# Query-by-query layout of the transposed tiles in a pre-norm retention and FP4-FFN layer

## The chip, the cores and the metric

The kernel runs on one core of one Trainium2 chip. The metric is the device time of one launch in microseconds. The core has five engines that run side by side and wait for each other through semaphores: TensorE (PE in the profile; its weight loads are the rows PEld), VectorE (DVE), ScalarE (ACT), GpSimd (POOL) and SyncE (SP), which here only issues DMAs.

## What is computed

The reference takes X of 8 sequences with 2048 rows of 256 values, all float32, and computes one layer:

```python
x = x + attn(layernorm(x), W_Q, W_K, W_V)
x = x + ffn(layernorm(x), w_gate, w_up, w_down)
# attn: Q = xpos(X @ W_Q); K = xpos(X @ W_K, downscale); V = X @ W_V
#       (softmax(Q K^T) * 0.9**|n-m|) @ V, softmax over all 2048 keys
# ffn:  down(silu(gate(x)) * up(x)); 704 hidden values; input and weights of each
#       linear are first rounded to FP4 (E2M1) values in blocks of 16
```

The decay 0.9**|n-m| is so small far from the diagonal that the kernel multiplies probabilities with V only in the key blocks at most 7 blocks of 128 away from the query block. The softmax's maximum and sum go over all keys.

## The kernel before

Work is done in blocks of 128 query rows (P = 128); there are 8 x 16 = 128 of them, and one call of `step(n)` for each. Groups of four blocks (GROUP = 512 rows) are loaded, normalized, transposed and projected ahead of time; keys and values of a whole sequence stay in SBUF. The instruction order of each engine is written out by hand in `step` (the tile framework's scheduling is set to manual), and the framework only adds the semaphores. A step works on several blocks at once, each at another stage. On block n it does the scores (`scores`, L474), the row maximum (`maximum`, L486) and the exponentials (`exponentials`, L507), and it turns the probabilities (`turn_p`). On block n-1 it multiplies the turned probabilities by the decay (`decays`, L547), multiplies them with V (`attend`, L562), adds the residual and normalizes (`add_residual`, `normal_scales`). On block n-2 it rounds the FFN input to FP4 and turns it (`turn_xq`), and runs the gate and up matmuls (`gate_up`, L630). On block n-3 it forms the hidden values, rounds them and turns them (`turn_h`). On block n-4 it runs the down matmuls (`down`, L678) and stores the result. On TensorE a step's order is: scores of n, projections of a later group, down of n-4, attend of n-1, gate and up of n-2. One matmul in float32 shows as two MATMUL and two LDWEIGHTS records in the profile.

TensorE multiplies with the contracted dimension on the partitions, so normalized x, probabilities, the FFN input xq and the hidden values h all have to be transposed. The function `turn` does this without TensorE. DVE's transpose (L238) turns squares of 32 x 32 (SQ = 32, NSQ = 4 squares along each side of a block) within groups of 32 partitions, out of the source into a scratch tile `sq`. ScalarE's queue then issues one DMA of `sq` to a DRAM tile `there` (L244), and SP issues four DMAs back (L247), which move the squares to the partitions where they belong; xq and h come back into the tile they came from. The turned data then lies in the order of the query's group of 32 first, then the block of values, then the query within its group: runs of 32 queries. `in_runs` is the view that names these runs.

Before TensorE uses them, x, xq and h are copied by ScalarE from that order into a tile with each block's 128 queries side by side: `keep_x` (L399, once for a group of four query blocks), `keep_xq` (L616) and `keep_h` (L669). For the probabilities the decay product on DVE (L547) reads the runs and writes the tile `p_t` with the queries side by side. The stationary operand of attend, gate, up and down is a slice of 128 queries of these tiles.

Three of the last blocks have their down matmuls put off to the very end (`deferred`); their turned h is kept in other tiles. The last few blocks are transposed by TensorE into PSUM instead (n of the last two for xq, of the last four for h, the last for the probabilities), and their copies read PSUM. Scores, projections, gate and up share three PSUM buffers (pool ps_s); attend and down share two (ps_m). The tiles h and xq have two buffers each. The changed lines are all in `turn`, the view after it, and the functions that use it.

Of the kernel before, what the change touches and what calls it, by code (L numbers as in the profile page):

```python
# [9 lines left out]
F32 = mybir.dt.float32  # L10
I32 = mybir.dt.int32
AF = mybir.ActivationFunctionType
ALU = mybir.AluOpType
AX = mybir.AxisListType

P = 128
GROUP = 512
BPG = GROUP // P
# [4 lines left out]
SQ = 32  # L23
NSQ = P // SQ
# [10 lines left out]
def preln_xpos_retention_fp4_ffn_kernel(  # L35
# [13 lines left out]
    nc = tc.nc  # L49
    B, L, H = x.shape  # L50
    F = w_gate.shape[0]
    HC = H // P
# [3 lines left out]
    FC = -(-F // P)  # L56
# [4 lines left out]
    ffn_p = ctx.enter_context(tc.tile_pool(name="ffn", bufs=2))  # L61
# [163 lines left out]

    def turn(dst, pieces, name, tag):


        n = sum(src.shape[-1] for src in pieces) // NSQ
        sq = prob_p.tile([P, dst.shape[-1]], F32, tag=tag, bufs=1, name=f"sq_{name}")
        sq = sq[:, : NSQ * n].rearrange("p (c f) -> p c f", c=NSQ)
        at = 0
        for src in pieces:
            w = src.shape[-1] // NSQ
            nc.vector.transpose(  # L238
                sq[:, :, at : at + w].rearrange("p c (k i) -> p k c i", i=SQ),
                src.rearrange("p (k c i) -> p k c i", c=NSQ, i=SQ),  # L240
            )
            at += w
        there = dram.tile([NSQ, SQ, NSQ, n], F32, tag=f"turn_{n}", name=f"there_{name}")
        nc.scalar.dma_start(there.rearrange("a i c f -> (a i) c f"), sq)  # L244
        dst = dst[:, : NSQ * n].rearrange("p (a f) -> p a f", a=NSQ)
        for c in range(NSQ):
            nc.sync.dma_start(dst[ts(c, SQ)], there[:, :, c, :].rearrange("a i f -> i a f"))  # L247

    def in_runs(t):

        return t.rearrange("p (a c i) -> p c a i", a=NSQ, i=SQ)

# [141 lines left out]
    def keep_x(k):  # L396
        xt = groups.pop(k).rearrange("p c d -> p (c d)")
        xn_t = act_p.tile([P, BPG, HC, P], F32, tag="xn_t", bufs=3, name=f"xnt_{k}")
        nc.scalar.copy(  # L399
            xn_t.rearrange("p b h (a i) -> p (b h) a i", a=NSQ), in_runs(xt)  # L400
        )
        normed[k] = xn_t
        load_group(k + 2)

# [117 lines left out]
    def turn_p(n):  # L522
        pieces = exps.pop(n)
        if n == total - 1:
            pt = ps_s.tile([P, HALF, P], F32, tag="s", name=f"pt_p_{n}")
            (pr,) = pieces
            for j in range(pr.shape[-1] // P):
                nc.tensor.transpose(pt[:, j, :], pr[:, ts(j, P)], ident)
            turned[n] = pt.rearrange("p k (a i) -> p k a i", a=NSQ)
        else:  # L530
            runs = prob_p.tile([P, (2 * BAND + 1) * P], F32, tag="runs", bufs=1, name=f"runs_{n}")
            turn(runs, pieces, f"p{n}", "sq")
            turned[n] = in_runs(runs[:, : len(band(n)) * P])


    mid = {}
# [1 line left out]
    def band(n):  # L538
        return [k for half in range(2) for k in keys_of(n, half)]

    def decays(n):
        keys, pt = band(n), turned[n]
        p_t = prob_p.tile([P, 2 * BAND + 1, P], F32, tag="p_t", bufs=1, name=f"p_t_{n}")
        d0 = keys[0] - n % NB + BAND
        for c in range(0, len(keys), BPG):
            to = min(c + BPG, len(keys))
            nc.vector.tensor_tensor(  # L547
                p_t[:, c:to, :].rearrange("p k (a i) -> p k a i", a=NSQ),
                pt[:, c:to],
                decay_sb[:, d0 + c : d0 + to, :].rearrange("p k (a i) -> p k a i", a=NSQ),  # L550
                ALU.mult,
            )
        turned[n] = p_t

# [48 lines left out]
    def turn_xq(n):  # L603
        xq = mid[n][1]
        if n >= total - 2:
            pt = ps_m.tile([P, HC, P], F32, tag="m", name=f"pt_xq_{n}")
            for hc in range(HC):
                nc.tensor.transpose(pt[:, hc, :], xq[:, ts(hc, P)], ident)
            keep_xq(n, pt.rearrange("p c (a i) -> p c a i", a=NSQ))
        else:  # L610
            turn(xq, [xq], f"xq{n}", "sq_x")

    def keep_xq(n, src=None):
        x1, xq, _ = mid[n]
        xq_t = ffn_p.tile([P, HC, P], F32, tag="xq_t", bufs=1, name=f"xq_t_{n}")
        nc.scalar.copy(  # L616
            xq_t.rearrange("p c (a i) -> p c a i", a=NSQ), in_runs(xq) if src is None else src
        )
        mid[n] = (x1, xq_t)

    gated = {}

# [29 lines left out]
    def turn_h(n):  # L652
        h = hid[n][1]
        if n >= total - 4:
            pt = ps_s.tile([P, FC + 2, P], F32, tag="s", name=f"pt_h_{n}")[:, :FC, :]
            for fc in range(FC):
                at = min(fc * P, F - P)
                nc.tensor.transpose(pt[:, fc, :], h[:, at : at + P], ident)
            keep_h(n, pt.rearrange("p c (a i) -> p c a i", a=NSQ))
        else:  # L660
            turn(h, [h[:, : (FC - 1) * P], h[:, F - P : F]], f"h{n}", "sq_h")

    def keep_h(n, src=None):
        x1, h, _ = hid[n]
        if n in deferred:
            h_t = deferred[n][:, : FC * P].rearrange("p (c q) -> p c q", c=FC)
        else:
            h_t = ffn_p.tile([P, FC, P], F32, tag="h_t", bufs=1, name=f"h_t_{n}")
        nc.scalar.copy(  # L669
            h_t.rearrange("p c (a i) -> p c a i", a=NSQ), in_runs(h) if src is None else src  # L670
        )
        hid[n] = (x1, h_t)

    def down(n):
# [67 lines left out]
    def step(n):  # L742
        on = lambda d: 0 <= n - d
        k = NG + n // BPG
        turn_group = (n == 1 or n % BPG == 0 and n > 0) and k < B * NG
        load_residual(n)
        scores(n, 0)
        if on(3):
            hidden(n - 3)
        if on(2):  # L750
            mid[n - 2][2].round()
        if on(3):
            hid[n - 3][2].largest()
        maximum(n, 0)
        weights_in_step(n, "maximum")
        scores(n, 1)
        if decays_first(n):
            decays(n - 1)
        if on(3):
            hid[n - 3][2].normalize()  # L760
        if on(4) and n - 4 < total - 4:
            keep_h(n - 4)
        if on(2):
            turn_xq(n - 2)
        maximum(n, 1)
        exponentials(n)
        if n == 1:
            turn_p(n)
        if on(2) and n - 2 < total - 2:
            keep_xq(n - 2)  # L770
        for g in kept:
            keep_x(g)
        kept.clear()
        weights_in_step(n, "exponentials")
        values = [(g, name) for name, g in parts(n) if name not in ROWS]
        project = lambda: [project_rotated(g, name) for name, g in parts(n) if name in ROWS]
        for g, name in values:
            project_v(g, name)
        if n != 2:
            project()  # L780
        for g, name in values:
            keep_v(g, name)
        if on(1) and not decays_first(n):
            decays(n - 1)
        for name, g in parts(n):
            if n == 1 and name in ROWS:
                rotate(g, name)
        if turn_group:
            if n in (1, BPG):
                statistics(k)  # L790
            normalize_on_scalar(k)
        weights_in_step(n, "decays")
        if on(3):
            hid[n - 3][2].round()
        if on(4) and n - 4 not in deferred:
            down(n - 4)
        if n == 2:
            attend(n - 1)
            project()
        for name, g in parts(n):  # L800
            if n != 1 and name in ROWS:
                rotate(g, name)
        if n > BPG and n % BPG == 1 and k + 1 < B * NG:
            statistics(k + 1)
        if n != 1 and n < total - 1:
            turn_p(n)
        if on(1) and n != 2:
            attend(n - 1)
        weights_in_step(n, "attend")
        for name, g in parts(n):  # L810
            if name in ROWS:
                load_tables()
        if on(4) and n - 4 not in deferred:
            finish(n - 4)
        if on(1):
            inverse_sum(n - 1)
        if n == total - 1:
            turn_p(n)
            decays(n)
            inverse_sum(n)  # L820
            attend(n)
        if on(1):
            add_residual(n - 1)
        if on(3) and n < total - 1:
            turn_h(n - 3)
        if turn_group:
            turn_x(k)
            kept.append(k)
        if on(1):
            normal_scales(n - 1)  # L830
        if on(2):
            gate_up(n - 2)
# [101 lines left out]
```

## Time and profile before

| what | value |
|---|---|
| time, median of 3 runs | 2886.91 us (2885.96 to 2888.23) |
| profiled execution: its time, its span | 2886.89 us, 2885.1 us |
| share of the span in which TensorE, DVE, POOL, ACT are busy | 98%, 86%, 49%, 37% |
| DVE transposes, busy (L238: p, h, xq, x) | 231.6, 138.2, 48.8, 34.4 us |
| DVE decay products, busy (L547) | 237.1 us |
| ACT copies of h, xq, x, busy (L669, L616, L399) | 106.4, 50.4, 29.2 us |
| TensorE's granted clock | 0.996 |

The profile is one execution, taken by the hardware profiler. An engine's busy time is the time in which at least one of its instructions runs; TensorE's matmuls are pipelined, so the busy time of PE is not its work at peak rate. In the rows of groups one finds line, engine, operation, the tiles written and read, the shapes, how many instructions, then the busy time in us and the mean of one in ns, and last the idle time of the engine just before them with what ended it. The view of waits gives for each pair of waiting and releasing instruction the time in total, how often, and the longest.

### The profile page before, as it was taken

What the parts mean: (1) busy time and instruction counts of PE and PEld (TensorE: products, weight loads), DVE (VectorE), ACT (ScalarE), POOL (GpSimd) and SP (SyncE); (2) the same over time, 40 slices, a digit from 0 to 9 for tenths busy, and PEclk for the clock granted to TensorE, in tenths of its full rate; (3) what the DMA queues carried; (4) which work ended last, traced back from release to release, by engine and by line L of the source; (5) the groups of instructions that cost most, each with busy time, mean ns of one, the idle gap of its engine ahead of it and who ended that gap; (6) DMA issues with size and microseconds to landing.
All of it is one profiled execution on the core that took longest, in us unless ns stands there. A gap on an engine that the chain in (4) does not pass through costs nothing. (4 is left out here: it accounts for less than half of the span.)

```text
span 2885.1 us, 34622 instructions
## 1 busy us (share of the span) xinstructions
PE 2822.0 (98%) x9702; PEld 1835.6 (64%) x9702; DVE 2479.2 (86%) x5636; ACT 1080.0 (37%) x1665; POOL 1414.6 (49%) x1329
## 2 busy tenths in 40 slices
PE   8899999999999999999999999999999999999988
PEld 5566666666666666666666666666666666666656
DVE  7898888888888888888888888888888888888877
ACT  3333343333433434433343334343334333333332
POOL 6554455444544454544454445544554544544442
PEclk9999999999999999999999999999999999999999
DMA  5455545555455545555546554555554555444541
GB/s 189 119 155 176 165 146 148 167 168 159 147 159 163 162 153 160 148 167 163 166 137 174 168 159 147 160 156 165 155 164 141 162 169 162 119 139 143 156 119 48
DMA packets 365761, 441.97 MB, mean 153 GB/s; under 512 B 102784, under 2 KB 313088, under 8 KB 365568
## 3 DMA queue, kind: packets, MB, share of 16 engines
q1 hardware_dynamic: 307248, 263.84, 35.2%
q10 hardware_dynamic: 58320, 175.92, 16.2%
q8 instruction: 76, 1.25, 0.2%
q14 instruction: 117, 0.96, 0.1%
HBM read 246.94 MB, written 192.68 MB: 152 GB/s over the span
## 5 line engine op out<-in xcount | busy, mean ns | idle before, releaser
L474 PE MATMUL s<-kt,qt 128*128 128x512 f32 x2048 | 901.9, 593 | 2.4 <-ACT h L642 1.1
L474 PEld LDWEIGHTS s<-kt,qt 128*128 128x128 f32 x2048 | 388.2, 190 | 460.2 <-issue 420.9
L562 PE MATMUL o<-v,p_t 128*128 128x256 f32 x2944 | 658.8, 380 | 6.8 <-DVE p_t L547 6.7
L562 PEld LDWEIGHTS o<-v,p_t 128*128 128x128 f32 x2944 | 560.6, 191 | 86.4 <-DVE p_t L547 8.5
L220 POOL TENSOR_TENSOR h<-h,big_h 128x704 f32<-128x704 f32 x126 | 212.2, 1684 | 519.4 <-DVE big_h L219 519.3
L642 ACT ACT_TABLE_LOAD x126 | 161.7, 1283 | 708.6 <-DVE xq L594 486.2
L669 ACT COPY h_t<-h 128x768 f32<-128x768 f32 x121 | 100.7, 832 | 803.0 <-DMA h<-there_h 803.0
L678 PE MATMUL d<-wd_t,h_t 128*128 128x256 f32 x1500 | 350.3, 383 | 27.3 <-ACT h_t L669 27.2
L678 PEld LDWEIGHTS d<-wd_t,h_t 128*128 128x128 f32 x1500 | 282.0, 191 | 108.4 <-ACT h_t L669 56.1
L486 DVE TENSOR_REDUCE m<-s 128x1 f32<-128x1024 f32 x256 | 309.5, 1209 | 40.0 <-PE s L474 39.5
L630 PE MATMUL gate<-wg_t,xq_t 128*128 128x352 f32 x1024 | 329.4, 465 | 9.1 <-ACT xq_t L616 9.0
L630 PE MATMUL up<-wu_t,xq_t 128*128 128x352 f32 x1024 | 323.8, 459 | 0.0
L507 ACT ACTIVATE p<-s,nmax 128x1024 f32<-128x1024 f32 x256 | 283.0, 1111 | 29.0 <-DVE nmax L491 27.5
L195 POOL TENSOR_TENSOR h<-h,inv_h 128x704 f32<-128x704 f32 x126 | 174.8, 1387 | 218.7 <-DVE inv_h L193 136.8
L630 PEld LDWEIGHTS up<-wu_t,xq_t 128*128 128x128 f32 x1024 | 194.6, 190 | 108.4
L630 PEld LDWEIGHTS gate<-wg_t,xq_t 128*128 128x128 f32 x1024 | 196.5, 193 | 101.8 <-ACT xq_t L616 11.4
L195 POOL TENSOR_TENSOR xq<-xq,inv_x 128x256 f32<-128x256 f32 x127 | 79.0, 622 | 361.3 <-DVE inv_x L193 175.4
L547 DVE TENSOR_TENSOR p_t<-runs,decay_sb 128x512 f32<-128x512 f32 (+3 forms) x414 | 237.1, 630 | 3.8 <-issue 1.1
L238 DVE STREAM_TRANSPOSE sq_p<-p 128x1024 f32<-128x1024 f32 (+7 forms) x239 | 223.7, 969 | 5.7 <-ACT p L507 5.7
L221 POOL TENSOR_TENSOR h<-h,big_h 128x704 f32<-128x704 f32 x126 | 211.9, 1682 | 9.9
L507 ACT ACT_TABLE_LOAD x125 | 160.4, 1283 | 99.0 <-DVE nmax L491 80.7
L220 POOL TENSOR_TENSOR xq<-xq,big_x 128x256 f32<-128x256 f32 x127 | 92.4, 727 | 201.3 <-DVE big_x L219 200.6
(164 smaller groups left out, 3522.4 us busy)
## 6 DMA issues: line engine op xcount, KB each, us to landing
there_h<-sq_h ACTq DMA_DIRECT2D x124, 384.0 KB, 3.3
h<-there_h SPq DMA_DIRECT2D x496, 96.0 KB, 3.9
rope_k<-in_rope_dram SPq DMA_DIRECT2D x32, 512.0 KB, 5.7
rope_q<-in_rope_dram SPq DMA_DIRECT2D x32, 512.0 KB, 5.7
xr<-in_L_attn_X_dram SPq DMA_DIRECT2D x128, 128.0 KB, 3.4
there_xq<-sq_xq ACTq DMA_DIRECT2D x126, 128.0 KB, 1.7
xq<-there_xq SPq DMA_DIRECT2D x504, 32.0 KB, 1.8
out_dram<-x SPq DMA_DIRECT2D x125, 128.0 KB, 5.2
```

The costliest lines, as they stand in the source:

```text
L195: self.wide_on.tensor_tensor(self.v3, self.v3, self.wide(inv), ALU.mult)
L220: self.wide_on.tensor_tensor(v, v, big, ALU.add)
L221: self.wide_on.tensor_tensor(v, v, big, ALU.subtract)
L238: nc.vector.transpose(sq[:, :, at : at + w].rearrange("p c (k i) -> p k c i", i=SQ), src.rearrange("p (k c i) -> p k c i", c=NSQ, i=SQ),)
L474: nc.tensor.matmul(ps[:, j, :], q[:, dc, ts(i % BPG, P)], kt[b, half * 2 + j][:, dc, :], start=(dc == 0), stop=(dc == 1),)
L486: nc.vector.tensor_reduce(raw_scores[n][:, half : half + 1], raw_scores[n, half], AX.XY, ALU.max)
L507: nc.scalar.activation(pr, raw_scores.pop((n, half)).rearrange("p j k -> p (j k)"), AF.Exp, bias=nmax, accum_out=sums[:, half : half + 1],)
L547: nc.vector.tensor_tensor(p_t[:, c:to, :].rearrange("p k (a i) -> p k a i", a=NSQ), pt[:, c:to], decay_sb[:, d0 + c : d0 + to, :].rearrang ...
L562: nc.tensor.matmul(po, p_t[:, j, :], vt[b, k // BPG][:, k % BPG, :], start=(j == 0), stop=(j == len(keys) - 1),)
L630: nc.tensor.matmul(ps[:, half, :FH], xq_t[:, hc, :], w[:, hc, ts(half, FH)], start=(hc == 0), stop=(hc == HC - 1),)
L642: nc.scalar.activation(h[:, :F].rearrange("p (j f) -> p j f", j=2), pss[0], AF.Silu)
L678: nc.tensor.matmul(pd, h_t[:, fc, :], wd_t[:, fc, :], start=(fc == 0), stop=(fc == FC - 1))
```

## The change

`turn` lays the turned data out in another order. In the scratch tile the transpose's result is no longer written as runs of 32 queries for each block of values; for each query the n values of the n blocks stand next to each other, so neighbouring queries of one block are n elements apart. n is the number of 128-wide blocks of the turned tile: 2 for xq, 6 for h, 8 for x, 8 to 15 for the probabilities. The DMAs to `there` and back are the same in number and in sizes. After them the tile is ordered query by query, and the new view `by_block` reads one block's 128 queries with a step of n elements.

With that, the FFN input and the hidden values are handed to the matmuls of `gate_up` and `down` as this view of the tile in which they came back; `keep_xq` and its copies are gone, and `keep_h` is left for the three deferred blocks and the last four. The copy of x by ScalarE stays and reads with a step of 8 elements. The decay product on DVE reads the probabilities with a step of n elements and writes as before. Line numbers of the changed kernel are up to 11 lower.

```diff
     def turn(dst, pieces, name, tag):
-        n = sum(src.shape[-1] for src in pieces) // NSQ
+        n = sum(src.shape[-1] for src in pieces) // P
         sq = prob_p.tile([P, dst.shape[-1]], F32, tag=tag, bufs=1, name=f"sq_{name}")
-        sq = sq[:, : NSQ * n].rearrange("p (c f) -> p c f", c=NSQ)
+        sq = sq[:, : P * n].rearrange("p (c f) -> p c f", c=NSQ)
+        blocks = sq.rearrange("p c (i k) -> p k c i", i=SQ)
         at = 0
         for src in pieces:
-            w = src.shape[-1] // NSQ
+            w = src.shape[-1] // P
             nc.vector.transpose(
-                sq[:, :, at : at + w].rearrange("p c (k i) -> p k c i", i=SQ),
-                src.rearrange("p (k c i) -> p k c i", c=NSQ, i=SQ),
+                blocks[:, at : at + w], src.rearrange("p (k c i) -> p k c i", c=NSQ, i=SQ)
             )
             at += w
-        there = dram.tile([NSQ, SQ, NSQ, n], F32, tag=f"turn_{n}", name=f"there_{name}")
+        there = dram.tile([NSQ, SQ, NSQ, SQ * n], F32, tag=f"turn_{n}", name=f"there_{name}")
         nc.scalar.dma_start(there.rearrange("a i c f -> (a i) c f"), sq)
-        dst = dst[:, : NSQ * n].rearrange("p (a f) -> p a f", a=NSQ)
+        dst = dst[:, : P * n].rearrange("p (a f) -> p a f", a=NSQ)
...
-    def in_runs(t):
-        return t.rearrange("p (a c i) -> p c a i", a=NSQ, i=SQ)
+    def by_block(t, n):
+        return t[:, : P * n].rearrange("p (q c) -> p c q", c=n)
...
     def keep_x(k):
-        nc.scalar.copy(
-            xn_t.rearrange("p b h (a i) -> p (b h) a i", a=NSQ), in_runs(xt)
-        )
+        nc.scalar.copy(xn_t.rearrange("p b h q -> p (b h) q"), by_block(xt, BPG * HC))
...
     def turn_p(n):
-            turned[n] = in_runs(runs[:, : len(band(n)) * P])
+            turned[n] = by_block(runs, len(band(n)))
...
     def decays(n):
             nc.vector.tensor_tensor(
-                p_t[:, c:to, :].rearrange("p k (a i) -> p k a i", a=NSQ),
-                pt[:, c:to],
-                decay_sb[:, d0 + c : d0 + to, :].rearrange("p k (a i) -> p k a i", a=NSQ),
-                ALU.mult,
+                p_t[:, c:to, :], pt[:, c:to, :], decay_sb[:, d0 + c : d0 + to, :], ALU.mult
             )
...
     def turn_xq(n):
             for hc in range(HC):
                 nc.tensor.transpose(pt[:, hc, :], xq[:, ts(hc, P)], ident)
-            keep_xq(n, pt.rearrange("p c (a i) -> p c a i", a=NSQ))
+            xq_t = ffn_p.tile([P, HC, P], F32, tag="xq_t", bufs=1, name=f"xq_t_{n}")
+            nc.scalar.copy(xq_t, pt)
         else:
             turn(xq, [xq], f"xq{n}", "sq_x")
-
-    def keep_xq(n, src=None):
...
+            xq_t = by_block(xq, HC)
+        mid[n] = (mid[n][0], xq_t)
...
     def turn_h(n):
             turn(h, [h[:, : (FC - 1) * P], h[:, F - P : F]], f"h{n}", "sq_h")
+            if n not in deferred:
+                hid[n] = (hid[n][0], by_block(h, FC))
...
     def step(n):
-        if on(4) and n - 4 < total - 4:
+        if n - 4 in deferred:
             keep_h(n - 4)
...
-        if on(2) and n - 2 < total - 2:
-            keep_xq(n - 2)
```

More of the change, by code (lines that the diff above doesn't have):

```diff
@@ L528, in turn_p @@
                 nc.tensor.transpose(pt[:, j, :], pr[:, ts(j, P)], ident)
-            turned[n] = pt.rearrange("p k (a i) -> p k a i", a=NSQ)
+            turned[n] = pt
         else:
@@ L608, in turn_xq @@
                 nc.tensor.transpose(pt[:, hc, :], xq[:, ts(hc, P)], ident)
-            keep_xq(n, pt.rearrange("p c (a i) -> p c a i", a=NSQ))
+            xq_t = ffn_p.tile([P, HC, P], F32, tag="xq_t", bufs=1, name=f"xq_t_{n}")
+            nc.scalar.copy(xq_t, pt)
         else:
             turn(xq, [xq], f"xq{n}", "sq_x")
-    def keep_xq(n, src=None):
[L614 to L619, printed above, removed]
+            xq_t = by_block(xq, HC)
+        mid[n] = (mid[n][0], xq_t)
     gated = {}
@@ L658, in turn_h @@
                 nc.tensor.transpose(pt[:, fc, :], h[:, at : at + P], ident)
-            keep_h(n, pt.rearrange("p c (a i) -> p c a i", a=NSQ))
+            keep_h(n, pt)
         else:
             turn(h, [h[:, : (FC - 1) * P], h[:, F - P : F]], f"h{n}", "sq_h")
+            if n not in deferred:
+                hid[n] = (hid[n][0], by_block(h, FC))
     def keep_h(n, src=None):
@@ L668, in keep_h @@
             h_t = ffn_p.tile([P, FC, P], F32, tag="h_t", bufs=1, name=f"h_t_{n}")
-        nc.scalar.copy(
-            h_t.rearrange("p c (a i) -> p c a i", a=NSQ), in_runs(h) if src is None else src
-        )
+        nc.scalar.copy(h_t, by_block(h, FC) if src is None else src)
         hid[n] = (x1, h_t)
```

## Prediction

> **What bounds the kernel now.** I read the page's busy times first.
>
> ```profile
> PE 2822.0 (98%) x9702; PEld 1835.6 (64%) x9702; DVE 2479.2 (86%) x5636; ACT 1080.0 (37%) x1665; POOL 1414.6 (49%) x1329
> ```
>
> TensorE (PE) is busy all the time and VectorE (DVE) is second, 405.9 us below the span of 2885.1. ScalarE (ACT), whose copies go, has 63% of the span free. So I asked next, in the view of who waits for whom, what TensorE loses; the columns are total us, times, longest.
>
> ```profile
> PE d L678 <- ACT h_t L669: 27.2, 33, 2.0
> PE gate L630 <- ACT xq_t L616: 9.0, 5, 3.0
> PE o L562 <- DVE p_t L547: 6.7, 2, 5.9
> ```
>
> The first two lines are all that the change can give back: 36.2 us. The same view for DVE says how firmly the second engine is tied to the first.
>
> ```profile
> DVE x L582 <- PE o L562: 120.1, 73, 4.2
> DVE xq L594 <- POOL rstd_f L159: 42.5, 38, 2.9
> DVE m L486 <- PE s L474: 39.5, 87, 0.7
> DVE h L648 <- ACT h L642: 29.8, 72, 0.7
> ```
>
> With the shorter rows of that view, DVE waits 185 us for PE, 58 for POOL, 36 for ACT and 17 for DMAs. Last, the groups with shapes kept apart, for the operations whose access pattern changes and those that price them (columns: busy us, mean ns of one; idle time before).
>
> ```profile
> L678 PEld LDWEIGHTS d<-wd_t,h_t 128*128 128x128 f32 x1500 | 282.0, 191 | 108.4 <-ACT h_t L669 56.1 <-issue 17.2
> L547 DVE TENSOR_TENSOR p_t<-runs,decay_sb 128x512 f32<-128x512 f32 x318 | 204.9, 694 | 3.8 <-issue 1.1
> L238 DVE STREAM_TRANSPOSE sq_p<-p 128x1024 f32<-128x1024 f32 x127 | 155.0, 1220 | 3.3 <-ACT p L507 3.3
> L238 DVE STREAM_TRANSPOSE sq_h<-h 128x640 f32<-128x640 f32 x124 | 104.8, 845 | 13.0 <-POOL h L222 12.3 <-DMA there_p<-sq_p 0.3 <-POOL qt L434 0.3
> L669 ACT COPY h_t<-h 128x768 f32<-128x768 f32 x121 | 100.7, 832 | 803.0 <-DMA h<-there_h 803.0
> L215 DVE SCALAR_TENSOR_TENSOR h<-h 128x704 f32<-128x704 f32 x128 | 113.0, 883 | 0.8 <-POOL h L195 0.8
> L219 DVE TENSOR_SCALAR big_h<-big_h 128x704 f32<-128x704 f32 x128 | 67.5, 527 | 4.4
> L616 ACT COPY xq_t<-xq 128x256 f32<-128x256 f32 x126 | 50.4, 400 | 55.9 <-DMA xq<-there_xq 53.3 <-POOL h L220 2.0
> L238 DVE STREAM_TRANSPOSE sq_x<-x 128x1024 f32<-128x1024 f32 x28 | 34.4, 1228 | 7.3 <-DMA there_p<-sq_p 6.8 <-ACT x L378 0.3
> L547 DVE TENSOR_TENSOR p_t<-runs,decay_sb 128x128 f32<-128x128 f32 x32 | 9.1, 283 | 0.0
> L238 DVE STREAM_TRANSPOSE sq_p<-p 128x128 f32<-128x128 f32 x16 | 4.5, 283 | 0.6 <-ACT p L507 0.6
> ```
>
> Every DVE row in question moves about one element per ns: decay products (694-283)/384 = 1.07 ns, transposes (1220-283)/896 = 1.046 ns.
>
> **The change, part by part.** The profiled execution took 2886.89 us, its span 2885.1, so 1.8 us lie around it; the median of the runs is 2886.91. I count on the span and add 1.8.
>
> *Removed: ScalarE's copies.* 121 of h (832 ns) and 126 of xq (400 ns) are 151 us of an idle engine, worth only what TensorE waited for them. The 33 waits at the down matmuls average 0.82 us, just one copy; without it TensorE waits for the DMA's landing itself, so a wait longer than a copy keeps its rest: I take 23 of the 27.2 us. The 5 gate waits average 1.8 us, so a 0.40 us copy gives back 2 of the 9.0. Gain 25 us, at most 36.
>
> *Added on TensorE's queue.* The changed program's order shows 476 more semaphore waits there, as four DMA landings replace one copy's end. Such a wait lasts 51 ns in the rows of the gate line: 24 us if none is hidden. Behind a late one stand attend or the next scores, as behind the copy before. Scores, which wait too, show 2.4 us idle in all over 2048, so I take 0; the net gain lies between 1 and 36.
>
> *Buffers.* h and xq are now held until their matmuls have read them. The silu that takes the h buffer again follows the gate matmuls, which stand behind that down on TensorE; the xq buffer is rewritten a step after its gate matmuls. No new wait: 0. DMAs, their sizes and all engines' orders stay as they were, except ScalarE's, without the copies.
>
> *Moved pattern 1: weight loads with a step.* xq is loaded with a step of 2 elements, h of 6 (24 bytes), 121 x 12 = 1452 loads. A load takes 191 ns and its matmul comes every 216 ns (the chain has 30 attend matmuls in 6.47 us), so up to 25 ns more is hidden. No weight load with a step is in the trace. Bounds: 0, and twice the time, 382-216 = 166 ns x 1452 = 241 us. I take 0, as the engine is no longer the bound below.
>
> *Moved pattern 2: DVE writes.* The transposes now write neighbouring values n elements apart: n is 6 for h, 8 for x, 8 to 15 for the probabilities (24 to 60 bytes), 2 for xq. Elements per partition: sq_p 127 x 1024 + 16 x (896+768+640+512+384+256+128) = 187,392, sq_h 124 x 768 = 95,232, sq_x 28 x 1024 = 28,672; sum 311,296.
>
> *Moved pattern 3: DVE reads.* The decay products read the probabilities with steps of 8 to 15 elements where they had runs of 32: 318 x 512 + 32 x (384+256+128) = 187,392 elements.
>
> *Price of a step.* The one stepped operand in the trace is read by ScalarE's copy at L140, with a step of 2 (view of that line; min/median/max ns):
>
> ```profile
> L140 ACT COPY wk_pair<-wk_raw x2: 424/426/428, 6.1 to 6.4; 128x256 f32<-128x256 f32 x2
> L140 ACT COPY wq_pair<-wq_raw x2: 417/418/420, 13.6 to 13.9; 128x256 f32<-128x256 f32 x2
> ```
>
> Against 400 ns for as many columns without a step (L616) it bounds the price from below: about nothing, and I use that for xq's step of 2. I exclude a gain: no operand becomes more regular. For the upper end there are rows where this engine's rate changes by how operands are fetched: L219 and L215 do the same 704 elements in 527 and 883 ns; with their 256-column forms (294 and 415 ns) 0.52 and 1.045 ns an element, a factor of 2. Another factor of 2 gives 2.1, which is also what GpSimd's two-operand products take in this trace ((1684-727)/448 = 2.14). [...] Reads +187,392 x 1.07 ns = 200.5 us, writes +311,296 x 1.046 = 325.6 us; both 526 us.
>
> [...]
>
> *Sum.* DVE busy 2479.2 + 526 = 3005 us: above the span, so DVE becomes the bound. Its idle time does not all go. Some 21 of its 128-fold groups show 4.3 to 4.5 us idle with no releaser (34 ns before each instruction that follows its own result): 92 us stay. The 185 us for PE go, since PE is then early. Of the 111 for POOL, ACT and DMAs between none and all stay: 3097 to 3208. I take a quarter, as the rstd_f trip (42.5) is mostly covered by longer sq_h transposes behind it: 3125, plus 1.8, **3127 us**. The 25 us that TensorE gains vanish in its new waits: scores will wait for score buffers that exponentials free late.
>
> **The rivals.**
>
> *Steps cost DVE nothing (faster).* For it: the L140 row, and that one element per ns may be the engine's own pace whatever the step. Then only TensorE's gain is left: 2887 - 25 = 2862 (2851 to 2886). It decides from below about 0.25 ns an element: 125 us spread over DVE's idle time beside PE.
>
> *One side pays, or both by half.* Reads alone: DVE 2680 + 92 + 111 = 2883, writes alone 2805 + 92 + 111 = 3008, both by half 2742 + 203 = 2945. DVE and PE are then near equal and collide step by step, as the band of keys changes each step's share: 2920 to 3010, middle 2960.
>
> *TensorE's loads pay, DVE doesn't.* The load of h grows past the 216 ns between matmuls. If only what a load streams doubles, say 128 columns at the 0.83 ns that 256 more moving columns cost in the rows of scores and attend ((593-380)/256), it is 298 ns: 82 x 1452 = 119 us, 2887 + 119 - 25 = 2981; all doubled, 3103. Against it: transposes issue every 114 ns with loads of 141 ns, so loads overlap.
>
> **How the numbers follow.** Both sides doubled 0.40 (3127, its own range 3097 to 3210); one side or half 0.25 (2960); nothing 0.29 (2862); loads alone 0.06 (2981). Faster by over 0.2% (about what a measurement here can tell, 6 us): the third case, 0.27 after its upper edge; same: 0.04, that edge and a partial price that just eats the gain; slower 0.69. Signs are mixed, so the range must reach from the third case to the first: 2851 to 3180, leaving the first's upper tail and full-price loads.
>
> **What would show it.** Right: sq_p 128x1024 near 2.2 us, p_t 128x512 near 1.25 us, sq_xq still 0.39; DVE above 95%, PE near 90% with waits at s. Load price: the PEld row of d<-wd_t,h beyond 191 ns and more than 2.6 us a tile. Wrong: those DVE rows unchanged with PE waiting for h<-there_h by a few us in all.

## The result and the profile after

The changed kernel takes 3092.49 us (median of 4 runs, 3092.22 to 3093.91) against 2886.43 us before (median of 4): a ratio of 1.0718, with a 95% interval of 1.0705 to 1.0731. It is 206 us slower, 34 us under the forecast of 3127 and inside its range of 2851 to 3180. The profiled execution has a span of 3090.4 us.

The page's busy times of the changed kernel:

```profile
PE 2907.2 (94%) x9702; PEld 1918.1 (62%) x9702; DVE 2817.6 (91%) x5636; ACT 963.9 (31%) x1418; POOL 1415.4 (46%) x1329
```

VectorE (DVE) has 338 us more to do with the same 5636 instructions, and TensorE (PE) is no longer busy all the time. The groups with shapes kept apart, of the operations whose access pattern changed (busy us, mean ns of one; idle time before). L544 was L547, L667 was L678, L398 was L399.

```profile
L667 PEld LDWEIGHTS d<-wd_t,h 128*128 128x128 f32 x1452 | 341.2, 311 | 109.8 <-issue 68.7 <-POOL h L195 24.2 <-POOL xq L222 9.0
L544 DVE TENSOR_TENSOR p_t<-runs,decay_sb 128x512 f32<-128x512 f32 x318 | 322.9, 1066 | 4.4 <-issue 0.8 <-DMA there_xq<-sq_xq 0.7 <-DMA runs<-there_p 0.3
L238 DVE STREAM_TRANSPOSE sq_p<-p 128x1024 f32<-128x1024 f32 x127 | 253.3, 1994 | 2.7 <-ACT p L504 2.7
L238 DVE STREAM_TRANSPOSE sq_h<-h 128x640 f32<-128x640 f32 x124 | 166.1, 1339 | 17.5 <-POOL h L222 17.5
L398 ACT COPY xnt<-x 128x1024 f32<-128x1024 f32 x28 | 57.9, 2068 | 0.1
L238 DVE STREAM_TRANSPOSE sq_x<-x 128x1024 f32<-128x1024 f32 x28 | 56.6, 2023 | 1.4 <-DMA there_p<-sq_p 1.1 <-ACT x L377 0.3
L238 DVE STREAM_TRANSPOSE sq_xq<-xq 128x256 f32<-128x256 f32 x126 | 49.0, 389 | 0.0
L544 DVE TENSOR_TENSOR p_t<-runs,decay_sb 128x128 f32<-128x128 f32 x32 | 12.0, 375 | 0.0
L238 DVE STREAM_TRANSPOSE sq_p<-p 128x128 f32<-128x128 f32 x16 | 6.2, 391 | 0.6 <-ACT p L504 0.6
```

The decay product went from 694 to 1066 ns, the transposes from 1220 to 1994 (p), 845 to 1339 (h) and 1228 to 2023 (x). The transpose of xq, written with a step of 2, stayed at 389 (387 before). Per element that is (1066-375)/384 = 1.80 ns for reads and (1994-391)/896 = 1.79 ns for writes, where 1.07 and 1.05 had been. Summed over all shapes the rows grew by 136 us (p_t), 141 (sq_p), 75 (sq_h) and 22 (sq_x), 374 us in all; DVE's busy time grew by 338, as neighbouring instructions on DVE overlap by 232 us in all where it was 183 before.

Who waits for whom, for TensorE and then for DVE (total us, times, longest):

```profile
PE s L471 <- ACT h L631: 79.2, 46, 2.7
PE d L667 <- DMA h<-there_h: 49.0, 39, 2.6
PE o L556 <- DVE p_t L544: 12.3, 20, 6.2
```

```profile
DVE h L637 <- ACT h L631: 60.8, 94, 1.0
DVE x L576 <- PE o L556: 24.8, 18, 3.2
DVE sq_h L238 <- POOL h L222: 17.5, 23, 1.3
DVE xq L588 <- POOL rstd_f L159: 8.4, 17, 2.1
DVE m L483 <- PE s L471: 1.7, 3, 0.8
```

The roles are exchanged, though not fully. DVE's waits for TensorE's attend and scores fell from 120.1 and 39.5 us to 24.8 and 1.7, so DVE is mostly the late one. It isn't busy all the time either: of the span of 3090.4 us DVE is idle for 273 us and TensorE for 183 (63 before). TensorE now waits for a score buffer that the silu (L631) has to free, and for h longer than it waited for the copy before (49.0 against 27.2 us), though no copy stands between.

### The profile page after: what moved, and what is told of

It is laid out like the page before. It is cut to its first block, busy times and chain, and to the rows that moved or that the text cites. A ratio compares the mean times of both kernels' runs of the same rounds, so it can differ in the third digit from the quotient of the medians.

```text
span 3090.4 us, 34858 instructions
## 1 busy us (share of the span) xinstructions
PE 2907.2 (94%) x9702; PEld 1918.1 (62%) x9702; DVE 2817.6 (91%) x5636; ACT 963.9 (31%) x1418; POOL 1415.4 (46%) x1329
## 5 line engine op out<-in xcount | busy, mean ns | idle before, releaser
L471 PE MATMUL s<-kt,qt 128*128 128x512 f32 x2048 | 949.2, 614 | 80.8 <-ACT h L631 79.2
L556 PE MATMUL o<-v,p_t 128*128 128x256 f32 x2944 | 663.4, 382 | 12.5 <-DVE p_t L544 12.3
L667 PE MATMUL d<-wd_t,h 128*128 128x256 f32 x1452 | 362.5, 400 | 59.6 <-DMA h<-there_h 49.0
L667 PEld LDWEIGHTS d<-wd_t,h 128*128 128x128 f32 x1452 | 341.2, 311 | 109.8 <-issue 68.7
L544 DVE TENSOR_TENSOR p_t<-runs,decay_sb 128x512 f32<-128x512 f32 (+3 forms) x414 | 372.7, 959 | 4.4 <-issue 0.8
L238 DVE STREAM_TRANSPOSE sq_p<-p 128x1024 f32<-128x1024 f32 (+7 forms) x239 | 356.4, 1559 | 4.6 <-ACT p L504 4.6
L619 PE MATMUL gate<-wg_t,xq 128*128 128x352 f32 x1008 | 324.5, 465 | 9.5 <-DMA xq<-there_xq 9.2
L619 PE MATMUL up<-wu_t,xq 128*128 128x352 f32 x1008 | 319.5, 460 | 0.0
L619 PEld LDWEIGHTS up<-wu_t,xq 128*128 128x128 f32 x1008 | 198.5, 197 | 101.3 <-issue 1.5
L619 PEld LDWEIGHTS gate<-wg_t,xq 128*128 128x128 f32 x1008 | 199.8, 199 | 94.2 <-issue 14.7
L238 DVE STREAM_TRANSPOSE sq_h<-h 128x640 f32<-128x640 f32 x248 | 194.4, 861 | 17.5 <-POOL h L222 17.5
```

Source lines behind the costliest of these rows:

```text
L238: nc.vector.transpose(blocks[:, at : at + w], src.rearrange("p (k c i) -> p k c i", c=NSQ, i=SQ))
L471: nc.tensor.matmul(ps[:, j, :], q[:, dc, ts(i % BPG, P)], kt[b, half * 2 + j][:, dc, :], start=(dc == 0), stop=(dc == 1),)
L544: nc.vector.tensor_tensor(p_t[:, c:to, :], pt[:, c:to, :], decay_sb[:, d0 + c : d0 + to, :], ALU.mult)
L556: nc.tensor.matmul(po, p_t[:, j, :], vt[b, k // BPG][:, k % BPG, :], start=(j == 0), stop=(j == len(keys) - 1),)
L619: nc.tensor.matmul(ps[:, half, :FH], xq_t[:, hc, :], w[:, hc, ts(half, FH)], start=(hc == 0), stop=(hc == HC - 1),)
L667: nc.tensor.matmul(pd, h_t[:, fc, :], wd_t[:, fc, :], start=(fc == 0), stop=(fc == FC - 1))
```

## The experiments

My theory after this: DVE's stepped writes and reads make the time, and both sides count. The rivals: TensorE's loads with a step and its direct waits for the landings make it; or one side of DVE alone does.

### The probabilities and x back to runs

```diff
-            turn(runs, pieces, f"p{n}", "sq")
-            turned[n] = by_block(runs, len(band(n)))
+            turn(runs, pieces, f"p{n}", "sq", "p c (k i) -> p k c i")
+            turned[n] = in_runs(runs[:, : len(band(n)) * P])
```

(Against the changed kernel; x in the same way, with the copy and the decay product of before. The new last argument of `turn` names the order in which the transposes write: `(k i)` is runs, `(i k)` is query by query.)

> The probabilities and x go back to runs of 32 queries; xq and h stay query by query and are loaded by TensorE with a step. Theory (VectorE's stepped accesses make the time): of VectorE's surcharge only the writes of sq_h remain, 124 x (494 + 114 ns) = 75 us, so VectorE is busy 2479 + 75 = about 2555 us, TensorE is the bound again, and the time is 2887 - 25 + 14 (the 226 instead of 216 ns between the stepped loads' matmuls, 1452 times), 2865 to 2890 us. Rival (TensorE's stepped loads and its direct waits for the landings make the time): these are all still there, so at least 3040 us.

Measured: 2898.56 us against 2891.79 before on that chip, a ratio of 1.0024 (1.0015 to 1.0033). DVE is busy 2546.0 us, close to the 2555 expected. Nearly all of the slowdown is gone while every stepped load of TensorE and every direct wait is still there: the TensorE rival falls. The time itself is 9 us over the expected range, on a chip where the kernel before took 5 us longer; the run with TensorE's step alone, below, puts most of the excess on the writes of sq_h that are left.

### The FFN tiles back to runs and copies

```diff
-            turn(xt, [xt], f"x{k}", "sq")
+            turn(xt, [xt], f"x{k}", "sq", "p c (i k) -> p k c i")
...
-            turn(runs, pieces, f"p{n}", "sq")
-            turned[n] = in_runs(runs[:, : len(band(n)) * P])
+            turn(runs, pieces, f"p{n}", "sq", "p c (i k) -> p k c i")
+            turned[n] = by_block(runs, len(band(n)))
```

(against the kernel before; `decays` and the copy of x as in the changed one)

> The reverse: xq and h go back to runs and to ScalarE's copies; probabilities and x stay query by query. Theory: VectorE keeps the surcharge of sq_p (239 x 590 ns = 141 us), sq_x (22 us) and p_t (136 us), busy about 2775 us, and the time is 2960 to 3050 us. Rival (TensorE's stepped loads and landing waits): both are gone, so 2870 to 2915 us.

Measured: 3059.92 us, a ratio of 1.0583 (1.0565 to 1.0600), DVE busy 2759.2 us; 10 us over the expected range. The part of the change that removes no copy at all, the layout of the probabilities and of x, makes most of the loss. Here TensorE's wait for the copy of h is 104.3 us where it was 27.2 before:

```profile
PE d L676 <- ACT h_t L667: 104.3, 83, 3.7
PE s L475 <- ACT h L640: 34.3, 30, 2.0
```

### The changed kernel with contiguous weight loads

```diff
-            xq_t = by_block(xq, HC)
+            xq_t = xq.rearrange("p (c q) -> p c q", c=HC)
...
-                hid[n] = (hid[n][0], by_block(h, FC))
+                hid[n] = (hid[n][0], h[:, : FC * P].rearrange("p (c q) -> p c q", c=FC))
```

> As the changed kernel, but TensorE loads xq and h from the same tiles in contiguous slices of 128 columns instead of with a step; this feeds the gate, up and down matmuls values in the wrong order, the work is the same. Theory: the loads fall from 312 to 191 ns and the spacing of the down matmuls from 226 to 216 ns, 14 us that lie beside VectorE: 3070 to 3093 us. Rival (the loads make the time): below 2950 us.

Measured: 3089.89 us, a ratio of 1.0680 (1.0664 to 1.0696). Loads of h fall to 196 ns on average and the spacing of the down matmuls from 224 to 216 ns (a chain of 12 of them from 2.68 to 2.59 us). The time moves by 3 us as it stands and by 0.4%, 11 us, in the ratios, which were taken on two chips; either way it is no more than the 12 us of spacing (8 ns, 1452 times). The loads are not the cause.

### TensorE's step alone

```diff
-            turn(xq, [xq], f"xq{n}", "sq_x")
+            turn(xq, [xq], f"xq{n}", "sq_x", "p c (k i) -> p k c i")
...
-            turn(h, [h[:, : (FC - 1) * P], h[:, F - P : F]], f"h{n}", "sq_h")
+            turn(h, [h[:, : (FC - 1) * P], h[:, F - P : F]], f"h{n}", "sq_h", "p c (k i) -> p k c i")
```

(against the first experiment's kernel)

> All four transposes write runs and the decay products read them, as before; only the loads of xq and h by TensorE keep the step, and ScalarE's two copies stay away. The tiles hold runs, so the gate, up and down matmuls get values in the wrong order; the work is the same. Theory: VectorE is back at 2479 us busy; what is left is TensorE's gain from the missing copies (25 us at most here) less 14 us for the 225 instead of 216 ns between down matmuls: 0 to 25 us under the kernel before. Rival (loads with a step and waiting for the landings cost more than they give): over the kernel before by 5 us or more, like the 7 us of the run with only the FFN tiles changed, whose excess would then not come from sq_h.

Measured: 2875.64 us against 2886.79 before, a ratio of 0.9965 (0.9952 to 0.9978): 11 us faster, near the 25 us of gain less 12 us of spacing. TensorE's wait for h is down to 5 us from the 27.2 us for its copy, and the loads take 310 ns.

```profile
PE d L671 <- DMA h<-there_h: 5.0, 6, 1.5
```

So the copies were worth about what the prediction took. The first experiment, which differs only by sq_h (and sq_xq) being written with a step, lies 17 us higher in the ratios' difference (0.0059): 65 us more busy time on DVE cost 17 of time, though DVE is idle for 351 us there.

### The changed kernel with contiguous reads in the decay product

```diff
-            turned[n] = by_block(runs, len(band(n)))
+            turned[n] = runs[:, : len(band(n)) * P].rearrange("p (c q) -> p c q", q=P)
```

> As the changed kernel, but the decay products read the probabilities' tile in contiguous slices; the products get values in the wrong order, the work is the same. Theory (both sides pay and add up on VectorE): p_t falls from 1066 back to 694 ns, VectorE to about 2685 us; between the runs at 2546 us busy (2897 us of span) and 2759 (3057) that is about 3000 us. Rival one (the writes alone make the time): 3075 us or more. Rival two (the reads alone): about 2890 us.

Measured: 2972.27 us, a ratio of 1.0297 (1.0279 to 1.0314), DVE busy 2682.8 us.

### The changed kernel with writes in runs

```diff
-        blocks = sq.rearrange("p c (i k) -> p k c i", i=SQ)
+        blocks = sq.rearrange("p c (k i) -> p k c i", i=SQ)
```

> As the changed kernel, but the transposes write runs of 32 as before, while everything else reads with the step; values are in the wrong order, the work is the same. Theory: sq_p falls from 1994 to 1220 ns, sq_h from 1339 to 845, VectorE to about 2590 us busy, and the time is 2900 to 2940 us. Rival one (the writes alone make the time): 2865 to 2890 us. Rival two (the reads alone): 3060 us or more.

Measured: 2961.31 us, a ratio of 1.0258 (1.0243 to 1.0274), DVE busy 2623.2 us. Both runs lie between all and nothing, so neither side alone makes the time: with stepped writes alone on DVE the kernel is 86 us slower than the kernel before, with stepped reads alone 75, and with both 206 (all three without the copies and with TensorE's step). That is more than the sum. It would fit if the first microseconds fell partly into DVE's idle time, which no run shows by itself. Both were off the expected figures, the reads' kernel by 21 us or more above and the writes' kernel by 28 below: with 60 us less to do on DVE the reads' kernel is only 11 us faster, so DVE's busy time does not fix the time alone. With the stepped reads alone (this run) DVE's idle time stands at other waits than in the full change:

```profile
DVE xq L588 <- POOL rstd_f L159: 71.0, 58, 2.9
DVE sq_h L238 <- POOL h L222: 43.9, 34, 2.1
```

In the kernel before the same two waits were 42.5 and 12.3 us, in the full change 8.4 and 17.5: with sq_h and sq_p written in runs DVE is early again for both of GpSimd's results, earlier even than before the change; why, no run shows.

### What a step costs by itself

Added after the last block of the kernel before, with the steps 1, 2, 3, 4, 5, 6, 8 and 15 (L885 to L892 for the products, the next eight lines for the transposes, the next eight for the copies, then L910 to L924 for the matmuls in every second line):

```diff
+    every = lambda s: flat[:, : P * s].rearrange("p (q c) -> p c q", c=s)[:, 0, :]
+    [nc.vector.tensor_tensor(out[:, j * P : j * P + P], every(4), flat[:, :P], ALU.mult) for j in four]
+    [nc.vector.transpose(sqs[:, : 512].rearrange("p (c i k) -> p k c i", c=NSQ, i=SQ)[:, :2], ...) for j in four]
+    [nc.scalar.copy(acts[:, j * P : j * P + P], every(4)) for j in four]
+    [nc.tensor.matmul(pst4, every(4), wd_t[:, 0, :], start=(j == 0), stop=(j == 5)) for j in range(6)]
```

> The kernel before, with work added after the last block: on operands with a step of 1, 2, 3, 4, 5, 6, 8 and 15 elements, four VectorE products of 128 columns read with the step, four transposes of 256 columns written with it, four ScalarE copies of 128 columns read with it, and one chain of six matmuls whose stationary operand has it. Its time is not to be compared. If the price comes from VectorE's access itself, the products stand near 283 ns at small steps and near 375 ns (1.79 ns an element) at 6 to 15 also here, where no other engine works; if it came from other engines' traffic in the changed kernel, all steps take 283 ns here. Where between 2 and 6 the price sets in, and whether at once or little by little, no run shows yet.

The view of each line, min/median/max in ns. DVE products read with a step of 1, 2, 3, 4 and 15:

```profile
L885 DVE TENSOR_TENSOR steps_out<-decay_sb x4: 281/284/286, 2890.5 to 2891.1; 128x128 f32<-128x128 f32 x4
L886 DVE TENSOR_TENSOR steps_out<-decay_sb x4: 284/284/285, 2891.3 to 2892.0; 128x128 f32<-128x128 f32 x4
L887 DVE TENSOR_TENSOR steps_out<-decay_sb x4: 309/318/322, 2892.2 to 2892.9; 128x128 f32<-128x128 f32 x4
L888 DVE TENSOR_TENSOR steps_out<-decay_sb x4: 359/367/377, 2893.1 to 2894.0; 128x128 f32<-128x128 f32 x4
L892 DVE TENSOR_TENSOR steps_out<-decay_sb x4: 352/354/355, 2897.9 to 2898.7; 128x128 f32<-128x128 f32 x4
```

DVE transposes written with 2, 3, 4 and 15, and TensorE loads with 2, 3, 4 and 6:

```profile
L894 DVE STREAM_TRANSPOSE steps_sq<-decay_sb x4: 446/446/447, 2900.9 to 2902.3; 128x256 f32<-128x256 f32 x4
L895 DVE STREAM_TRANSPOSE steps_sq<-decay_sb x4: 529/534/540, 2902.8 to 2904.5; 128x256 f32<-128x256 f32 x4
L896 DVE STREAM_TRANSPOSE steps_sq<-decay_sb x4: 646/654/655, 2905.1 to 2907.1; 128x256 f32<-128x256 f32 x4
L900 DVE STREAM_TRANSPOSE steps_sq<-decay_sb x4: 611/611/612, 2915.9 to 2917.8; 128x256 f32<-128x256 f32 x4
L912 PEld LDWEIGHTS steps_m<-wd_t,decay_sb x12: 195/196/197, 2892.7 to 2895.0; 128*128 128x128 f32 x12
L914 PEld LDWEIGHTS steps_m<-wd_t,decay_sb x12: 251/252/253, 2895.3 to 2897.6; 128*128 128x128 f32 x12
L916 PEld LDWEIGHTS steps_m<-wd_t,decay_sb x12: 308/329/332, 2897.8 to 2900.4; 128*128 128x128 f32 x12
L920 PEld LDWEIGHTS steps_m<-wd_t,decay_sb x12: 309/309/313, 2903.4 to 2905.8; 128*128 128x128 f32 x12
```

The price is there with the rest of the kernel finished. A step of 2 elements costs nothing on DVE (284 ns as at 1 for 128 elements read, 446 as at 1 for 256 written) and 6 ns on a load (196 where 1 takes 190); 3 costs 34 ns for 128 elements read, (534-446)/256 = 0.34 ns an element written; at the steps from 4 to 15 the price stays about level: 70 to 84 ns for 128 elements read (354 to 368 ns), 0.64 to 0.81 ns an element written (611 to 654 ns). ScalarE's copies show the same edge (292 ns at 1, 304 at 2, 360 at 3, 423 at 4, 413 to 428 above).

The added work did not run one engine at a time, as the expectation had it: ScalarE's copies and TensorE's loads read the same tile with their steps beside the products (the last copy starts at 2899.2 us, the last matmul at 2911.7). Only the transposes after that ran beside neither, 636 ns at a step of 8 and 611 at 15 against 446 at 1, so for writes the price is DVE's own. For reads two runs above show it: without DVE's step but with TensorE's (the first experiment, first line) the decay product is as fast as before the change, and with DVE's step but without TensorE's (the second, next line) it has the whole price.

```profile
L547 DVE TENSOR_TENSOR p_t<-runs,decay_sb 128x512 f32<-128x512 f32 x318 | 205.5, 696 | 4.3 <-DMA there_xq<-sq_xq 0.7 <-issue 0.4 <-DMA xr<-in_L_attn_X_dram 0.4
L548 DVE TENSOR_TENSOR p_t<-runs,decay_sb 128x512 f32<-128x512 f32 x318 | 320.3, 1057 | 3.8 <-issue 1.1
```

The pace of about one element per ns, which the prediction's first rival took as possibly the engine's own whatever the step, does not hold here: 1.79 ns an element against 1.05.

### The silu ahead of the turned h

```diff
+        if on(2):
+            gate_up(n - 2)
         if on(3) and n < total - 1:
             turn_h(n - 3)
...
-        if on(2):
-            gate_up(n - 2)
```

(against the changed kernel)

> The changed kernel with one more move: at the end of a step the gate and up matmuls and the silu stand ahead of turning h, so that on ScalarE's queue the silu no longer stands behind the DMA issue that waits for sq_h. Theory (VectorE is the bound, and of its 273 us of idle time the 61 us spent waiting for the silu come from that place in ScalarE's queue): VectorE's wait for h falls below 15 us and the time to 3020 to 3050 us. Rival (that wait is only what another would take over): 3080 to 3100 us. If the later issue of h's DMA makes TensorE wait longer for its landing, that wait rises above the 49 us it has now.

Measured: 3035.47 us, a ratio of 1.0512 (1.0497 to 1.0528): 57 us faster than the changed kernel, with DVE as busy as there (2814.9 us). DVE's wait for the silu and the scores' wait for its buffer are both gone from the longer waits, and DVE is idle for 219 us in place of 273. This shows where a part of DVE's idle time came from. On ScalarE's queue the issue of h's DMA waits for sq_h, and the silu of the next block stood behind it; DVE and, for a buffer, the scores then waited for the silu. One such place in the changed kernel, first DVE, then ScalarE (start us, us, engine, line, operation, times, idle time before):

```profile
1516.05 1.55 DVE L238 STREAM_TRANSPOSE sq_h<-h 128x640 f32<-128x640 f32 x2
1520.26 0.89 DVE L637 TENSOR_TENSOR h<-up,h 128x704 f32<-128x704 f32 x1 [0.69 <-ACT h L631]
1517.63 0.36 ACTq L243 DMA_DIRECT2D there_h<-sq_h  x1
1518.17 1.28 ACT L631 ACT_TABLE_LOAD   x1 [8.12 <-PE s L471]
1519.47 0.76 ACT L631 ACTIVATE h<-gate 128x704 f32<-128x704 f32 x1
```

The other side of the move also showed: h's DMA is issued later, and TensorE waits 83.4 us for its landing in place of 49.0.

```profile
PE d L667 <- DMA h<-there_h: 83.4, 59, 2.5
PE o L556 <- DVE p_t L544: 12.9, 8, 6.2
```

### xq alone

```diff
-            turn(xq, [xq], f"xq{n}", "sq_x")
+            turn(xq, [xq], f"xq{n}", "sq_x", "p c (i k) -> p k c i")
+            mid[n] = (mid[n][0], xq.rearrange("p (q c) -> p c q", c=HC))
...
-        if on(2) and n - 2 < total - 2:
-            keep_xq(n - 2)
```

(against the kernel before)

> The kernel before with xq alone query by query (a step of 2 elements) and without ScalarE's copy of it; h, x and probabilities as before. Theory (a step of 2 costs nothing on any engine): VectorE stays at 2479 us busy, the gate loads take 196 ns and their matmuls still come every 296 ns, and only TensorE's wait at gate (9 us, 5 times) shrinks: 0 to 5 us under the kernel before. Rival (waiting for the landing itself costs what the copy cost): no change or up to 5 us over.

Measured: 2878.76 us against 2886.67 before, a ratio of 0.9972 (0.9961 to 0.9984): 8 us faster, and the one version here that computes the whole layer and beats both kernels. Gate loads take 197 ns, and the gate matmuls still come every 296 ns. The gain is a little over the 5 us expected at most: the gate's wait fell from 9.0 to 6.0 us, the wait at the down matmuls from 27.2 to 24.1. What the other 2 us are is open.

### h in pairs

```diff
+        sq = sq.rearrange("p (c g i j) -> p j g c i", c=NSQ, g=3, j=2)
+        for j in range(2):
+            src = h[:, START[3 * j] : START[3 * j] + 3 * P]
+            nc.vector.transpose(sq[:, j], src.rearrange("p (g c i) -> p g c i", c=NSQ, i=SQ))
...
+            for g in range(3):
+                half = there[:, :, c, ts(g, 2 * SQ)].rearrange("a i f -> i a f")
+                nc.sync.dma_start(dst[ts(c, SQ), g], half)
```

(against the first experiment's kernel; the six blocks start at 0, 128, 256, 320, 448 and 576, and the zeroed rows of the down weights move to the fourth block)

> A version meant to keep the gain without the price: xq query by query, probabilities and x in runs, and the six 128-wide blocks of h turned as three pairs, each query by query, so that both the transposes' writes and TensorE's loads step by 2 elements. Its price is the way back from DRAM: 12 DMAs a block with pieces of 256 bytes in place of 4 with 768. Theory: sq_h takes about 0.86 us in two transposes of 384 columns, loads 196 ns, down matmuls come every 216 ns: 10 to 25 us under the kernel before. Rival (the 8 further DMA issues, 0.43 us each on SP's queue, and the smaller pieces make h land later): TensorE waits at the down matmuls for longer than the 27 us that it waits for the copy before, and nothing is won or some is lost.

Measured: 3075.62 us, a ratio of 1.0655 (1.0640 to 1.0669). DVE's accesses are free as planned: the two transposes take 558 ns each (not the 430 expected), as much as the 845 and 269 ns before, and DVE is busy 2473.9 us. The loads take 217 ns on average (median 197). And yet it is nearly as slow as the full change. One of the issues for h holds SP's queue for 0.43 us in the median (0.30 to 1.48), so a block's 12 hold it for about 5.2 us, an estimate from that median, where a group of 4 took 1.73 to 1.85 us between 1499 and 1530 us of this run, and TensorE waits for the landing. One of the long ones:

```profile
1519.25 8.35 SPq L268 DMA_DIRECT2D h<-there_h  x12
```

```profile
PE d L696 <- DMA h<-there_h: 131.2, 61, 5.2
```

DVE then waits for TensorE (275 us at the attend results alone). Whether the number of issues or the smaller pieces do it was not separated. The step of 6 in h could not be avoided cheaply this way.

## Why the prediction was right, and where it was not

**DVE becomes the bound.** Right in the direction and for the reason given: stepped writes and reads. Putting the probabilities and x back, or either side of DVE's accesses, takes the loss away in parts; taking TensorE's step away does not. The sign named for it was missed: DVE was to be above 95% busy and TensorE near 90%; they are at 91% and 94%. DVE is the one that is waited for more, but it still waits itself, and the two hold each other up.

**The size of a step's price** failed. The step "another factor of 2 gives 2.1" was the term of 526 us. No run shows that doubling, an estimate of mine from the rates of other instructions; the runs show a factor of 1.7 (1.79 ns), 374 us by the rows and 338 in DVE's busy time. The rows taken for the upper end (0.52 and 1.045 ns an element at L219 and L215, and GpSimd's 2.14) priced other things and say nothing of a step.

**What DVE idles beside its work** failed the other way. The forecast left 120 us of idle time; 273 stayed. "The 185 us for PE go": 45 stayed. "I take a quarter" of the 111 for POOL, ACT and DMAs: none of it went, as ACT rose from 36 to 66, POOL fell from 58 to 29 and DMAs went from 17 to 19. And the idle time that the view puts down to no wait is 113 us, not 92 (109 before). The named wait was right: the trip of rstd_f went from 42.5 to 8.4 us. The largest missing one was the silu, queued on ScalarE behind a DMA issue that waits for a transpose which had itself become slower: 29.8 to 60.8 us for DVE, 79.2 for TensorE's scores. The forecast did have scores wait for buffers, but for ones that the exponentials free late. Of ScalarE's queue the prediction weighed only the copies, not what a late DVE would hold up there. So 3127 came out only 34 us off by luck: two errors offset each other, 188 us too much work (526 against 338) and 153 too little idle time.

**TensorE's gain of 25 us and the load's price.** The gain held in the run with TensorE's step alone (11 us with 12 of spacing taken off). In the changed kernel it went in new waits, as forecast: TensorE waits 49.0 us for h. The load was taken at 0 beyond 191 ns; it takes 311, more than the 216 between matmuls, yet the matmuls only spread to 224: loads overlap, as the transposes' rows (141 ns each, one every 114) had suggested for the rival. In the changed kernel this is worth at most the 3 to 11 us that contiguous loads gave back.

**The 476 further semaphore waits** were taken at 0, and the run with TensorE's step alone leaves room for little more: it gained 11 us where the waits and the spacing alone give about 13.

**One access was overlooked:** ScalarE's copy of x reads with a step of 8 elements and went from 1041 to 2068 ns, 29 us on an engine that is 31% busy. TensorE's wait for it did not grow (1.6 us before, 0.8 now).

**The rival with one side** had the right range (2920 to 3010), but its sums for each side (2883 for reads, 3008 for writes) missed the measured 2961 and 2972. For the reads the busy time was even less than its sum had (2623 against 2680), and DVE idles 336 us there: the waits made that difference, not the busy time.

## What to carry to other kernels

Before a layout is changed to save a copy, price every other engine that reads or writes the tile: here the saved copies were worth 25 us on TensorE, and the same helper put a step into the accesses of the second-busiest engine. In these runs a step of 2 float32 elements is free on VectorE (284 ns for 128 elements read, as without a step) and one of 4 to 15 makes its work up to 1.7 times as long (1.79 ns an element against 1.05), so a layout with two blocks side by side can be loaded by TensorE directly (8 us gained with xq alone) and one with six or fifteen should not be touched by VectorE. When the second engine becomes the bound, look at what is queued behind its results on a third engine: moving one call there gave back 57 of 206 us. And late input to TensorE can cost as much as a slower VectorE: with h in pairs DVE had no more to do than before, and the kernel was still 189 us slower.

## What was not expected of the hardware

TensorE's pace fell after a wait. In the changed kernel's timeline (start us, us, engine, line, operation, times, then the idle time before) eight records of score matmuls take 3.60 us, and the next eight, after 2.35 us of waiting, 5.40:

```profile
1514.33 3.60 PE L471 MATMUL s<-kt,qt 128*128 128x512 f32 x8
1520.28 5.40 PE L471 MATMUL s<-kt,qt 128*128 128x512 f32 x8 [2.35 <-ACT h L631]
```

The granted clock is 1.00 in the first stretch (1514.3 to 1518 us), 0.70 in the second (1520.2 to 1525.8) and 1.00 again in the 4 us behind it; over the whole changed kernel it is 0.981, where it was 0.996 before. So this wait of 2.35 us was followed by 1.8 us lost to a lower clock. All scores together are 47 us longer than before (949.2 against 901.9 us busy) beside 79.2 us of waits. With the silu moved ahead those waits are gone and the pace is back (first the changed kernel, then that run):

```profile
L471 PE MATMUL s<-kt,qt 128*128 128x512 f32 x2048 | 949.2, 614 | 80.8 <-ACT h L631 79.2
L471 PE MATMUL s<-kt,qt 128*128 128x512 f32 x2048 | 900.2, 592 | 1.4 <-DVE h L637 1.4
```

A part of that run's 57 us may thus be TensorE's pace and not DVE's wait. TensorE's busy time grew by 85 us in the changed kernel (2822.0 to 2907.2) with the same 9702 matmul records, and its idle time by 120. How much of the 206 us the clock is by itself is open, since no run took all of TensorE's waits away and left the rest.

That a weight load of 311 ns fits between matmuls 224 ns apart was also more overlap than I had taken for granted.
